# A four-layer graph network: the queries of layers 2 and 3 made with the keys and values, kept in DRAM, and loaded already replicated

## The chip, the core and the metric

The kernel runs on one core of a Trainium2 chip. The metric is the device time of one execution in microseconds; three runs of the kernel before took 2970.14 to 2981.36 us, with a median of 2976.62. The engines are called PE (TensorE, matmuls; PEld are its weight loads), DVE (VectorE), ACT (ScalarE), POOL (GpSimd) and SP (SyncE, which here only issues DMAs).

## What is computed

16 graphs share one adjacency matrix of 1024 nodes with about 8 neighbours each. Every node has 128 features in each graph, in float32. Four layers follow each other: attention (8 heads of 16) with a feed-forward part, a graph attention layer, and two more attention layers like the first.

```python
# attention layer (L0, L2, L3), for each of the 16 graphs
Q, K, V = h @ Wq, h @ Wk, h @ Wv                  # 8 heads of 16
scores = Q . K / sqrt(16), over neighbours only
attn_out = softmax(scores) @ V
x = layer_norm(h + attn_out @ Wo + bo) * ln1_g + ln1_b
y = relu(x @ W1 + b1) @ W2 + b2                   # 128 -> 256 -> 128
x = layer_norm(x + y) * ln2_g + ln2_b

# graph attention layer (L1)
h = x @ W;  e = leaky_relu(h @ a_src + (h @ a_dst)^T), over neighbours only
x = layer_norm(softmax(e) @ h + x) * ln_gamma + ln_beta
```

## The kernel before

**Units.** The nodes are sorted by degree and cut into T = 8 tiles of 128. The 16 graphs form two groups (g) of 8, and each group two halves (h) of GH = 4. A unit is one layer, group and tile; 64 units run one after another, layer by layer, group by group.

**Parts.** The work of a unit is gathering. For each tile there is a list of chunks; a chunk is 128 neighbour slots, 4 slots of 32 destination nodes each, and the 8 tiles have 17, 12, 12, 11, 8, 8, 8 and 6 chunks. In an attention layer a part is two chunks, in the graph layer four. For a part, GpSimd gathers rows of keys and values (8 graphs x 128 features x 2) from a table in DRAM with indirect DMAs (`gathered`, L746), three parts ahead, into four buffers. VectorE multiplies keys by queries (`products`, L757), adds up each head (`exponentials`, L773), ScalarE takes the exponential (L777), and VectorE multiplies the values by it (`weighted`, L798). TensorE adds the slots of a node together with 0/1 matrices (`summed`, L825).

**Queries.** Partition p of a chunk belongs to destination node p mod 32 of a block j of 32. The queries must therefore stand in SBUF four times over, `qr[32*s + n, j, :]`, for s = 0 to 3. `queries(u + 1)` does that while unit u runs. For each half: four matmuls with Wq (L718), a ScalarE copy to the tile `q` (L722), four matmuls with a 0/1 matrix that repeats 32 rows four times (L727), and four ScalarE copies of 128x512 from PSUM to `qr` (L730). The tile `q` comes from a pool with one buffer, `qr` from one with two.

**Tails.** When all parts of a unit are summed, `divided` makes the quotients, and two tails (one for each half) carry them on while the next unit's parts run: output projection, norm, feed-forward part, norm, and, in `finish`, the transposed result and `project` of the next layer. `project` stores the transposed state in DRAM (`kept`, L456; loaded again by `loaded` two units ahead), multiplies it by Wk and Wv (L464), copies the result to `kv` (L468), and stores that in the next layer's table (L473). The second half runs one step behind the first.

**Order.** Everything is emitted in an order written out by hand, with Python generators; each `yield` is one step. Each engine works through its own instructions in that order. `others()` is called three or four times for a part: it advances both tails by a step at a pace of STEPS (GRAPH_STEPS in layer 1) steps per unit, and one generator of `fronts` (queries and loads of the next units) or, if there is none, of `slow`. What is left of the tails at the end of the next unit is emitted at once (`while tails`), and so are the `fronts` at the end of each unit.

**The slow path.** While group 0 of layer 0 runs, `at_leisure(1)` makes the keys and values of group 1: for each of 16 half tiles it loads `xg` (one buffer, L620), transposes it (L522), runs `project` for layer 0 and stores the table. Before the first gather of group 1 what remains of it is emitted at once.

All DMAs from SP (loads of x, xg and weights, stores of kept and tables) are issued in one queue; the gathers are issued by GpSimd.

Of the kernel before, what the change touches and what calls it, by code (L numbers as in the profile page):

```python
# [12 lines left out]
F32 = mybir.dt.float32  # L13
# [7 lines left out]
P = 128  # L21
D = 128
# [18 lines left out]
N = 1024  # L41
T = N // P
GR = 2
G = B // GR
HF = 2
GH = G // HF
ROW = G * D
# [13 lines left out]
            CHUNK[_t, _r, _j] = len(CHUNK)  # L61
NC = len(CHUNK)

STEPS = 16
GRAPH_STEPS = 9
AHEAD = 3

# [9 lines left out]
def sparse_path(ctx: ExitStack, tc: tile.TileContext, a: dict, out: bass.AP, flag):  # L77
# [9 lines left out]
    def bank(shape):  # L87
        return banks.tile(shape, F32, tag="ps", name="ps")
# [351 lines left out]
    for l, (_, names) in enumerate(LAYERS):  # L440
# [5 lines left out]
        (l, g): dram.tile([T, P, HF, GH * P], F32, name=f"kept{l}{g}")  # L446
        for l in range(1, len(LAYERS)) for g in range(GR)
    }
    xs = {}
    srcs = {}  # L450


    def project(l, g, t, h, x, kv=None):

        if l:
            nc.sync.dma_start(kept[l, g][t, :, h, :], x.rearrange("p g n -> p (g n)"))  # L456
        table = tables[l, g][t * P : (t + 1) * P, :]
        if LAYERS[l][1] is ATTN:
            if kv is None:
                kv = twos.tile([P, 2, GH, D], F32, tag="kv", name="kv")  # L460
            for i in range(0, GH, 2):
                ps = bank([P, 2, 2 * D])
                for k in range(2):
                    nc.tensor.matmul(  # L464
                        ps[:, k, :], x[:, i + k, :], w[LAYERS[l][0], "Wkv"],
                        start=True, stop=True,
                    )
                nc.scalar.copy(  # L468
                    kv[:, :, i : i + 2, :].rearrange("p c g d -> p g c d"),
                    ps.rearrange("p g (c d) -> p g c d", d=D),  # L470
                )
                yield
            nc.sync.dma_start(  # L473
                table.rearrange("p (c x) -> p c x", c=2)[:, :, h * GH * D : (h + 1) * GH * D],
                kv.rearrange("p c g d -> p c (g d)"),
            )
            return
        kv = twos.tile([P, GH * D + GH], F32, tag="kv", name="kv")
        if h == 0:
            srcs[g, t] = const.tile([P, G], F32, name=f"src{g}{t}")  # L480
        for i in range(0, GH, 2):
            ps = bank([P, 2, D + 2])
            for k in range(2):
                nc.tensor.matmul(ps[:, k, :], x[:, i + k, :], wg, start=True, stop=True)
            nc.scalar.copy(
                kv[:, i * D : (i + 2) * D].rearrange("p (g d) -> p g d", d=D), ps[:, :, :D]
            )
            to = GH * D + i
            nc.scalar.copy(
                kv[:, to : to + 2].rearrange("p (g o) -> p g o", o=1), ps[:, :, D : D + 1]  # L490
            )
            at = h * GH + i
            nc.scalar.copy(
                srcs[g, t][:, at : at + 2].rearrange("p (g o) -> p g o", o=1), ps[:, :, D + 1 :]
            )
            yield

        nc.sync.dma_start(table[:, h * GH * D : (h + 1) * GH * D], kv[:, : GH * D])
        nc.sync.dma_start(table[:, ROW + h * GH : ROW + (h + 1) * GH], kv[:, GH * D :])
# [30 lines left out]

    def finish(l, g, t, h, z, gain, shift):
        if l + 1 < len(LAYERS):
            xn = states.tile([P, GH, P], F32, tag="xT", name="xT")
            turned(z, xn, gain, shift)
            yield
            yield from project(l + 1, g, t, h, xn)
            return
        o = twos.tile([P, GH, D], F32, tag="kv", name="outs")
        nc.gpsimd.tensor_tensor(o, z, over_graphs(gain), ALU.mult)
        nc.gpsimd.tensor_tensor(o, o, over_graphs(shift), ALU.add)  # L540
        nc.gpsimd.indirect_dma_start(
            out=out.rearrange("n (k c) -> (n k) c", k=GR * HF),
            out_offset=bass.IndirectOffsetOnAxis(ap=places[:, g, h, t : t + 1], axis=0),
            in_=o.rearrange("p g d -> p (g d)"), in_offset=None,
        )
# [59 lines left out]
    def natural(g, t, h, rows, kv=None):  # L605

        xn = states.tile([P, GH, P], F32, tag="xT", name="xT")
        turned(rows, xn)
        yield
        yield from project(0, g, t, h, xn, kv)  # L610

    def columns(g, h, n=1):
        at = (g * HF + h) * GH * D
        return slice(at, at + n * GH * D)

    def at_leisure(g):
        def fetch(k):
            rows = ones_.tile([P, GH, D], F32, tag="xg", name="xg")
            if k < T * HF:
                nc.sync.dma_start(  # L620
                    rows.rearrange("p g d -> p (g d)"),
                    a["x"][k // HF * P : (k // HF + 1) * P, columns(g, k % HF)],
                )
            return rows

        rows = fetch(0)
        yield
        for k in range(T * HF):
            steps = natural(g, k // HF, k % HF, rows)
            next(steps)  # L630
            rows = fetch(k + 1)
            yield
            yield from steps

    def at_once(g):

# [66 lines left out]
    def queries(u):  # L703

        l, g, t = units[u]
        if not is_attention(u):
            ps = bank([P, J, G])
            for j in range(J):
                nc.tensor.matmul(ps[:, j, :], rep_of(j, True), srcs[g, t], start=True, stop=True)
            ofs[u] = smalls.tile([P, J, G], F32, tag="of", name="of")  # L710
            nc.scalar.copy(ofs[u], ps)
            return
        qs[u] = reps.tile([P, J, ROW], F32, tag="qr", name="qr")
        for h in range(HF):
            q = ones_.tile([P, GH * D], F32, tag="q", name="q")
            ps = bank([P, GH, D])
            for i in range(GH):
                nc.tensor.matmul(  # L718
                    ps[:, i, :], xs[l, g, t][:, h, i, :], w[LAYERS[l][0], "Wq"],
                    start=True, stop=True,  # L720
                )
            nc.scalar.copy(q, ps.rearrange("p g d -> p (g d)"))  # L722
            yield
            pss = []
            for j in range(J):
                ps = bank([P, GH * D])
                nc.tensor.matmul(ps, rep_of(j), q[32 * j : 32 * j + 32], start=True, stop=True)  # L727
                pss.append(ps)
            for j in range(J):
                nc.scalar.copy(qs[u][:, j, h * GH * D : (h + 1) * GH * D], pss[j])  # L730
            yield
# [133 lines left out]
    def advance(gens):  # L865
        for gen in list(gens):
            if next(gen, "end") == "end":
                gens.remove(gen)

    pace = [0.0, 0.0]  # L870

    def others():
        pace[0] += pace[1]
        while pace[0] >= 1.0:
            advance(tails)
            pace[0] -= 1.0
        for gens in (fronts or slow,):
            if gens and next(gens[0], "end") == "end":
                gens.pop(0)

# [528 lines left out]
```

## Time and profile before

| | |
|---|---|
| runs of the kernel before, median (range) | 2976.62 us (2970.14 to 2981.36) |
| the profiled execution, its own time | 2966.73 us |
| span of that execution | 2965.0 us, mean granted clock 0.832 |
| busy, share of the span | PE 71%, PEld 44%, DVE 72%, ACT 48%, POOL 51% |
| chain of waits that ended last, by engine | PE 30%, ACT 11%, DVE 11%, POOL 9%, issue 7%, DMA 4% |
| DMA | 611.19 MB, mean 206 GB/s; gathers 45.1% of 16 engines, SP's transfers 11.5% |
| copies qr<-ps, L730 (all three attention layers) | 384, busy 197.5 us, mean 596 ns |
| matmuls ps<-q,rep, L727 | 768 records, busy 168.9 us |
| matmuls ps<-Wq,x, L718 | 768 records, busy 116.0 us |

In the tables of groups, a row is one line, engine and operation: the tiles, the count, busy time and mean, then the idle time of the engine just ahead of it and what ended that. A float32 matmul leaves two records. In rows of waits the three numbers are the total in us, how often, and the longest. In a timeline the first number is the start in us from the start of the span, the second how long it took, and brackets hold the idle time before it. Rows of DMA issues give the count, the size and the median time from issue to landing.

### The profile page before, as it was taken

Reading aid. Unit: us, or ns where it says so; the run is one execution under the profiler, and the core shown is the slowest. Engines: PE = TensorE matmul, PEld = TensorE weight load, DVE = VectorE, ACT = ScalarE, POOL = GpSimd, SP = SyncE. Lnnn points to the kernel's source line nnn. Section 1 sums busy time; section 2 is a strip of 40 time slices with the busy share of each in tenths; the row PEclk is TensorE's granted clock in tenths of the full one; section 3 lists DMA queues with packets and bytes.
Section 4 is the critical chain, followed back from the end, with each engine's and each line's share of the span. In section 5 each row is a group of like instructions: output and inputs, shape, how many; then the busy total and the mean of one; then the engine's idle time right before and its main releaser. Section 6 shows DMA issues by size and latency. Waiting matters only on the chain.

```text
span 2965.0 us, 35574 instructions
## 1 busy us (share of the span) xinstructions
PE 2097.9 (71%) x12692; PEld 1316.6 (44%) x12692; DVE 2141.1 (72%) x1521; ACT 1427.9 (48%) x4482; POOL 1517.5 (51%) x1096
## 2 busy tenths in 40 slices
PE   6466677767687867766587886778777676666766
PEld 5334445434454534333255553455534344334444
DVE  7876656478766566667788768886688876788772
ACT  3134455544556545345255653555644455334454
POOL 3334443354555587784254433444435566466673
PEclk8677788887788988978789988889987888777887
DMA  7655555366464577787566555565565454365540
GB/s 244 247 191 188 198 204 179 118 218 244 157 242 143 190 269 263 282 280 290 186 240 253 195 200 229 224 248 206 185 238 210 181 204 181 119 238 206 189 146 23
DMA packets 168842, 611.19 MB, mean 206 GB/s; under 512 B 44216, under 2 KB 47672, under 8 KB 120158
## 3 DMA queue, kind: packets, MB, share of 16 engines
q0 software_dynamic: 100736, 485.12, 45.1%
q1 hardware_dynamic: 67920, 123.71, 11.5%
q8 instruction: 102, 1.67, 0.2%
q14 instruction: 84, 0.69, 0.1%
HBM read 654.87 MB, written 92.34 MB: 252 GB/s over the span
## 4 chain that ended last, share of the span: by engine, by line
PE 30%; ACT 11%; DVE 11%; POOL 9%; issue 7%; DMA 4%; POOLq 0%; DVEq 0%; SPq 0%; ACTq 0%
PE ps L572 6%; ACT z L506 4%; PE yps L581 4%; PE acc L825 4%; PE ps L522 4%; POOL e L746 4%; DVE pr L798 3%; DVE sc L773 3%; POOL rstd L512 3%; DMA e<-table,idx 3%; DVE pr L757 3%; PE ps L464 2%; ACT qr L730 2%; PE yps L585 2%; PE yps L558 2%
## 5 line engine op out<-in xcount | busy, mean ns | idle before, releaser
L746 POOL DMA_INDIRECT e<-table,idx x656 | 894.3, 1363 | 456.1 <-DVE pr L798 257.8
L798 DVE TENSOR_TENSOR pr<-e,ex 128x2048 f32<-128x2048 f32 (+1 forms) x344 | 760.0, 2216 | 414.8 <-ACT ex L777 409.3
L512 POOL TENSOR_TENSOR rstd<-total,power 128x4 f32<-128x4 f32 x224 | 371.1, 1658 | 688.0 <-ACT z L506 645.8
L757 DVE TENSOR_TENSOR pr<-e,qr 128x2048 f32<-128x2048 f32 (+1 forms) x258 | 565.6, 2192 | 101.2 <-DMA e<-table,idx 62.9
L825 PE MATMUL acc<-pr,marks 128*32 128x512 f32 x2624 | 467.1, 692 | 154.3 <-DVE pr L798 143.8
L773 DVE TENSOR_REDUCE sc<-pr 128x128 f32<-128x2048 f32 (+1 forms) x258 | 561.7, 2177 | 0.0
L522 PE MATMUL ps<-ident,z 128*128 128x128 f32 x768 | 196.1, 366 | 215.2 <-ACT z L515 215.2
L522 PEld LDWEIGHTS ps<-ident,z 128*128 128x128 f32 x768 | 126.8, 172 | 360.6 <-ACT z L515 291.6
L825 PEld LDWEIGHTS acc<-pr,marks 128*32 128x32 f32 x2624 | 89.6, 119 | 408.4 <-issue 212.8
L464 PE MATMUL ps<-Wkv,xT 128*128 128x256 f32 x768 | 227.3, 440 | 57.9 <-ACT xT L524 39.5
L572 PE MATMUL ps<-x,W 128*128 128x512 f32 x384 | 240.0, 758 | 38.3 <-ACT x L526 38.3
L581 PE MATMUL yps<-W,f 128*128 128x128 f32 x1536 | 257.3, 285 | 12.8 <-ACT f L576 10.6
L581 PEld LDWEIGHTS yps<-W,f 128*128 128x128 f32 x1536 | 210.8, 195 | 69.9 <-ACT f L576 43.6
L576 ACT ACTIVATE f<-ps,b 128x512 f32<-128x512 f32 x192 | 131.4, 687 | 228.3 <-PE ps L572 227.6
L730 ACT COPY qr<-ps 128x512 f32<-128x512 f32 x384 | 197.5, 596 | 76.8 <-PE ps L727 76.6
L506 ACT ACTIVATE z<-y,root 128x128 f32<-128x128 f32 x512 | 198.5, 396 | 48.3 <-DVE y L599 37.2
L777 ACT ACTIVATE ex<-sc 128x128 f32<-128x128 f32 (+1 forms) x258 | 81.2, 315 | 287.3 <-DVE sc L773 287.1
L727 PE MATMUL ps<-q,rep 32*128 32x512 f32 x768 | 168.9, 679 | 63.8 <-ACT oT L524 39.1
L464 PEld LDWEIGHTS ps<-Wkv,xT 128*128 128x128 f32 x768 | 157.0, 218 | 99.0 <-ACT xT L524 43.0
L558 PE MATMUL yps<-Wo,oT 128*128 128x128 f32 x768 | 179.9, 321 | 8.7 <-ACT oT L524 8.7
L515 ACT ACTIVATE z<-y,rstd 128x128 f32<-128x128 f32 x512 | 162.6, 391 | 24.7 <-POOL rstd L512 24.7
L559 PE MATMUL yps<-centre,x 128*128 128x128 f32 x768 | 170.4, 309 | 0.0
(148 smaller groups left out, 2922.4 us busy)
## 6 DMA issues: line engine op xcount, KB each, us to landing
table<-kv SPq DMA_DIRECT2D x88, 512.0 KB, 9.1
kept<-xT SPq DMA_DIRECT2D x96, 256.0 KB, 5.3
x<-kept SPq DMA_DIRECT2D x48, 512.0 KB, 9.8
e<-table,idx POOLq DMA_INDIRECT x656, 7.5
table<-kv SPq DMA_DIRECT2D x32, 256.0 KB, 6.4
edges<-in_adj SPq DMA_DIRECT2D x8, 512.0 KB, 6.0
spare<-in_x SPq DMA_DIRECT2D x8, 512.0 KB, 7.7
table<-ex SPq DMA_DIRECT2D x8, 512.0 KB, 7.8
```

Of the source, the lines that this page charges most:

```text
L464: nc.tensor.matmul(ps[:, k, :], x[:, i + k, :], w[LAYERS[l][0], "Wkv"], start=True, stop=True,)
L506: nc.scalar.activation(z[:, i, :], y[:, i, :], AF.Square, scale=D**-0.5, bias=root, accum_out=total[:, i : i + 1],)
L512: nc.gpsimd.tensor_tensor(rstd, total, power, ALU.pow)
L522: nc.tensor.transpose(ps[:, i, :], z[:, i, :], ident)
L572: nc.tensor.matmul(ps, p["W1"][:, f * P : (f + 1) * P], x1.rearrange("p g n -> p (g n)"), start=True, stop=True,)
L581: nc.tensor.matmul(ps[:, i, :], f1[:, f, i * P : (i + 1) * P], p["W2"][:, f, :], start=(f == 0), stop=False,)
L730: nc.scalar.copy(qs[u][:, j, h * GH * D : (h + 1) * GH * D], pss[j])
L746: nc.gpsimd.indirect_dma_start(out=es[i][:, k, :], out_offset=None, in_=tables[l, g][:, :], in_offset=bass.IndirectOffsetOnAxis(ap=idx[:, ...
L757: nc.vector.tensor_tensor(prs[i][0][:, :n, :], es[i][:, :n, :ROW], qs[u][:, j : j + n, :], ALU.mult)
L773: nc.vector.tensor_reduce(sc[:, :n, :], prs[i][0][:, :n, :].rearrange("p k (a d) -> p k a d", d=HD), mybir.AxisListType.X, ALU.add,)
L798: nc.vector.tensor_tensor(prs[i][k0 // 2][:, :m, :].rearrange("p k (a d) -> p k a d", d=d), es[i][:, k0 : k0 + m, base : base + ROW].rearr ...
L825: nc.tensor.matmul(accums[u][32 * j : 32 * j + 32, h, :], marks[:, CHUNK[t, r, j], :], tiles[j // 2][:, j % 2, h * GH * D : (h + 1) * GH * D],
```

## The change

In layers 2 and 3 the queries are no longer made just ahead of their unit. `project`, in the tail of the layer before, multiplies its state by Wq as well, copies the result to `q` and stores it in a table `qtab` in DRAM. `queries` then fills `qr` by 16 loads of 32 rows of 4 KB, four copies of each block, issued by SP. Layer 0 makes its queries as before. STEPS goes from 16 to 17, since `project` has one more step; GRAPH_STEPS stays. Two flags are added around the slow path: `held` is set while `at_leisure` is inside a half tile, and `busy` counts the tails that are inside `finish`. `finish` first advances the slow path while `held` is set, and `others` takes the slow path only if it is inside a half tile or no tail is in `finish`.

```diff
-STEPS = 16
+STEPS = 17
...
+    qtabs = {
+        (l, g): dram.tile([N, ROW], F32, name=f"qtab{l}{g}")
+        for l, (_, names) in enumerate(LAYERS) if l and names is ATTN for g in range(GR)
+    }
...
@@ project
+            if l:
+                q = ones_.tile([P, GH * D], F32, tag="q", name="q")
+                ps = bank([P, GH, D])
+                for i in range(GH):
+                    nc.tensor.matmul(
+                        ps[:, i, :], x[:, i, :], w[LAYERS[l][0], "Wq"], start=True, stop=True
+                    )
+                nc.scalar.copy(q, ps.rearrange("p g d -> p (g d)"))
+                yield
+                nc.sync.dma_start(
+                    qtabs[l, g][t * P : (t + 1) * P, h * GH * D : (h + 1) * GH * D], q
+                )
             return
...
@@ finish
         if l + 1 < len(LAYERS):
+
+            while held[0]:
+                advance(slow)
+            busy[0] += 1
             xn = states.tile([P, GH, P], F32, tag="xT", name="xT")
             turned(z, xn, gain, shift)
             yield
             yield from project(l + 1, g, t, h, xn)
+            busy[0] -= 1
             return
...
+    busy, held = [0], [False]
+
@@ at_leisure
         for k in range(T * HF):
             steps = natural(g, k // HF, k % HF, rows)
+            held[0] = True
             next(steps)
             rows = fetch(k + 1)
             yield
             yield from steps
+            held[0] = False
...
@@ queries
         qs[u] = reps.tile([P, J, ROW], F32, tag="qr", name="qr")
+        if l:
+            for j in range(J):
+                at = t * P + 32 * j
+                rows = qtabs[l, g][at : at + 32, :]
+                for s in range(S):
+                    nc.sync.dma_start(qs[u][32 * s : 32 * s + 32, j, :], rows)
+            return
...
+    def idle():
+        return slow if held[0] or not busy[0] else []
+
     def others():
...
-        for gens in (fronts or slow,):
+        for gens in (fronts or idle(),):
             if gens and next(gens[0], "end") == "end":
                 gens.pop(0)
```

## The prediction

> **What bounds the kernel now.** I read the granted clock and span first (one core, 2965.0 us, clock 0.832), then busy time by stage. The starts of VectorE's RECIPROCAL, one per unit, give the layers: layer 0 runs to about 975 us, layer 1 to 1370, layer 2 to 2150, layer 3 to 2935. Busy time of each engine in these four stretches (PE, PEld, DVE, ACT, POOL, then the clock, the DMA share and GB/s):
>
> ```profile
> 110.00:975.00 865.00, 595.61 (x3595) 385.76 (x3595) 592.63 (x404) 412.40 (x1319) 390.57 (x266) 0.81 0.53 190
> 975.00:1370.00 395.00, 287.61 (x1948) 163.84 (x1948) 250.37 (x271) 184.77 (x636) 285.46 (x214) 0.87 0.75 262
> 1370.00:2150.00 780.00, 588.84 (x3516) 364.87 (x3516) 612.44 (x359) 421.01 (x1258) 334.39 (x249) 0.86 0.59 218
> 2150.00:2935.00 785.00, 542.07 (x3181) 333.80 (x3181) 600.86 (x340) 362.69 (x1174) 461.49 (x327) 0.82 0.49 182
> ```
>
> No engine is full. In layers 2 and 3 VectorE leads with 77 to 79%, in layer 1 the DMA engines with 75%. Next, who VectorE and ScalarE wait for; first layer 0, then layer 3:
>
> ```profile
> DVE pr L798 <- ACT ex L777: 227.0, 52, 13.7
> ACT kv L485 <- DMA table<-kv: 45.5, 5, 14.5
> ...
> DVE pr L798 <- ACT ex L777: 76.8, 32, 5.6
> DVE pr L757 <- DMA e<-table,idx: 45.8, 19, 5.5
> ```
>
> VectorE's largest wait is for the exponentials, a 0.3 us activation. It is late because ScalarE works through one queue, and copies and norms of the tail stand ahead of it. The second line is a warning for this change: a ScalarE copy stood up to 14.5 us, with all behind it, until a store had read the buffer it was to fill.
>
> One part (two chunks) costs VectorE three instructions of 2.2 us, 6.6 us. A unit of tiles 1 to 3 has 6 parts and so 39.6 + 3.2 us (reciprocal, two quotients, two sums) = 42.8 us; a unit of tiles 4 to 6 has 4 parts, 29.6 us; the measured units are 47.7 and 40 to 42 us in layer 2, 50 to 52 and 41 to 42 in layer 3. So large units hang on VectorE with 5 to 8 us of stalls, and small ones on the tail: a chain of TensorE, ScalarE and GpSimd steps spread over the unit. How the queries stand in that chain, in the timeline of a small unit of layer 3:
>
> ```profile
> 2462.45 2.05 ACT L730 COPY qr<-ps 128x512 f32<-128x512 f32 x4 [0.47 <-PE ps L727]
> ...
> 2468.16 2.02 ACT L730 COPY qr<-ps 128x512 f32<-128x512 f32 x4
> ...
> 2470.05 0.34 ACT L777 ACTIVATE ex<-sc 128x128 f32<-128x128 f32 x1
> ...
> 2479.18 0.69 ACT L576 ACTIVATE f<-ps,b 128x512 f32<-128x512 f32 x1 [3.00 <-PE ps L572]
> ...
> 2482.35 2.29 DVE L798 TENSOR_TENSOR pr<-e,ex 128x2048 f32<-128x2048 f32 x1 [3.55 <-ACT ex L777]
> ```
>
> The second group of four copies holds up the tail's next norm step by 2 us; 12 us later the tail is late, ScalarE waits 3.00 us for TensorE in it, and VectorE loses 3.55 us behind that.
>
> The boundary of two units in layer 2, where the change puts its new copies:
>
> ```profile
> 1644.54 0.21 ACT L844 COPY both<-ps 128x64 f32<-128x64 f32 x1 [2.55 <-PE ps L839]
> ...
> 1648.00 0.59 ACT L524 COPY oT<-ps 128x512 f32<-128x512 f32 x1
> ...
> 1649.33 0.31 ACT L777 ACTIVATE ex<-sc 128x128 f32<-128x128 f32 x1
> ```
>
> And what a store takes to land in layer 2 (last number, median us), and the slow path's loads in layer 0:
>
> ```profile
> table<-kv SPq DMA_DIRECT2D x32, 512.0 KB, 12.6
> kept<-xT SPq DMA_DIRECT2D x33, 256.0 KB, 5.4
> ...
> xg<-in_x SPq DMA_DIRECT2D x12, 256.0 KB, 4.1
> ```
>
> [...]
>
> **The change part by part.**
>
> *Removed in layers 2 and 3* (32 units): the repeating matmuls (16 records a unit; by stretch 53.5 us in layer 2 and 58.3 in layer 3, 3.5 us a unit) and the copies to qr (8 a unit, 66.9 and 62.0 us, 4.0 a unit). *Moved one layer up*: the Wq matmuls (16 records, 2.3 us a unit) and the copy q (two of 0.585 us) go into the tail of layers 1 and 2. Net: layer 3 loses 5.8 us of TensorE and 5.2 of ScalarE a unit, layer 2 loses the repeating part, layer 1 gains 2.3 and 1.2 us.
>
> *Layer 3.* In the unit shown, the tail reaches the scaled z of its first half earlier by 0.8 (Wq ahead of Wo on TensorE) + 0.7 (first copies ahead of the squares) + 0.6 (copy q) + 2.1 (second copies) = about 4 us. In small units I give VectorE that and half a microsecond of late sums, 4.5 us: 8 x 4.5 = 36. In tiles 1 to 3 only the one stall of about 2.7 us per unit on ex goes, the others are GpSimd's outs and gathers: 6 x 2.5 = 15. In the two large units 4 each, 8. Sum -59. Against it the loads: 16 transfers of 128 KB a unit, 2 MB. They may start when VectorE is done with the products of the unit before last, a whole unit ahead, when GpSimd is busy with outs and gathers are few. By the layer's rate when busy (182 GB/s at a share of 0.49, 371 GB/s) 2 MB are 5.7 us of all DMA engines. A landing gather may be that much later, once a unit; three parts of prefetch hide most. I take 0.7 us a unit, 11 us; bounds 0 and 5 us a unit (80). Layer 3: -48.
>
> *The new wait.* The tile q has one buffer. Both halves of a tail come one step apart, so in ScalarE's queue the second half's copy q stands one kv copy after the first half's, and must wait until the first half's q store has landed. Behind it stand the next unit's oT (the start of its tail), of, and ex; VectorE waits for these. Landing: 2.0 us at least, 5.4 as for kept[...]. I take 8 us in layer 2, 5.5 in layer 1 (there kept lands in 3.7 and the 512 KB store in 7.8).
>
> *Layer 2.* From "both" at 0: first q ready at 1.9, store issued 2.2, landed 10.2, second q 10.8, oT 11.4, ex 11.8. VectorE can use ex from 6.8 (reciprocal, quotients, reduction, products), so it loses 5 us, and the tail starts 8 us later than at 1648.00. Minus the 4 us that the queries' leaving saves in the tail: +4 in small units (8 x 4 = 32); +3.5 in tiles 1 to 3, where 1.5 is saved (6 x 3.5 = 21); +3 twice in the large ones (6). The three waits of VectorE for qr copies in this layer, 22.0 us, go but for 4: -18. Layer 2: +41; with the bounds on the landing -25 to +90.
>
> *Layer 1.* Small units (15 to 22 us) are led by the tail, whose step count GRAPH_STEPS stays at 9 although it has one yield more, so the end is flushed at the unit's border. There q waits about 5 us ahead of "of", on which VectorE's next scores depend: 8 x 5 = 40. In the other eight units VectorE waits for gathers anyway (56.5 us in the layer), and I take 1 us for q and 1 for the 0.5 MB more stored per unit: 16, less 1 hidden. Layer 1: +55; bounds +15 and +100.
>
> *Layer 0.* The flag held is set at each tile's start and cleared only when the generator is resumed, which at once sets it again for the next tile; no yield lies between. So the loop in finish does not end one tile, it drains the slow path to its end. In the changed instruction order 13 transposes of xg stand in one block on TensorE in unit 1, ahead of the first kept store. One tile's period there: transposes 1.1, issue 0.5, landing of the next xg 4.1 plus what the 512 KB store beside it takes, 6.5 us in all (5.3 with the shortest landing of 3.6, 10 with the longest, 9.1). 12 x 6.5 + 5 for the last tile - 6 that VectorE still has queued = 77 us stall. In return the other units lose this work: tiles 1 to 7 take 605.78 - 198.27 = 407.5 us in group 0 and 1003.72 - 672.43 = 331.3 in group 1, which has none: -76. Layer 0: +1; bounds -15 and +45.
>
> Sum: +1 + 55 + 41 - 48 = +49 us on the profiled execution (2966.73 us, span 2965.0), 3016. The runs' median, 2976.62, stands 10 us above that: 3026.
>
> **The rivals.** What this measurement can tell from no change is about 0.5%, 15 us.
> 1. *Relief wins* (ends faster). The q store lands in 3 to 4 us[...]; layer 1 costs 25, layer 2 gains 10, layer 3 gains 65, layer 0 gains 5: -55, 2922. It decides from a landing under 4.5 us on. For it: kept lands in 3.7 in layer 1, 2.0 at best. Against: the 512 KB store just ahead.
> 2. *The pieces cancel.* Landing about 6 us and layer 1's waits mostly behind gathers: within 15 us, 2977.
> 3. *Transfers collide with gathers.* The 2 MB a unit delay gathers by 2 us or more each unit: +64 on the forecast, 3090. For it: the DMA wait of 45.8 us in layer 3 is already there. Against: layer 1 runs at 262 GB/s with only 56.5.
> 4. *A long drain.* At 10 us a tile the block is 119 us: +42, 3068.
>
> **How the numbers follow.** Forecast (3000 to 3055) 0.37, relief 0.20, cancel 0.13, collision 0.17, long drain 0.13. Faster 0.20, same 0.13, slower 0.67. Range 2932 to 3092.
>
> **What would show it.** A stretch of 65 to 100 us in unit 1 of layer 0 with VectorE idle for ex, then units of 55 and 44 us; a wait of ScalarE's q for the qtab DMA, 32 times, 3 to 8 us; layer 1 longer by 15 to 100 us; small units of layer 3 near 37 us. I am wrong if that wait is under 3 us, if unit 1 shows no block, or if layer 3 does not shorten.

## The result, and the profile after

| | runs | median us (range) | ratio to before (95% interval) |
|---|---|---|---|
| before | 4 | 2973.80 (2970.14 to 2981.36) | |
| after | 4 | 3142.78 (3138.92 to 3157.20) | 1.0574 (1.0533 to 1.0615) |

The changed kernel is slower by 169 us. The forecast was 3026 us in a range of 2932 to 3092: the direction is right, the size is not. The profiled execution of the changed kernel took 3140.48 us, its span is 3138.7 us and the mean granted clock 0.804 (before: 0.832).

First the stages. The starts of VectorE's RECIPROCAL, one a unit, cut both traces into layers. This table gives the length of each layer in us, and the mean unit of tiles 1 to 3 and of tiles 4 to 7:

| | layer 0 | layer 1 | layer 2 | layer 3 | units of layer 2 | units of layer 3 |
|---|---|---|---|---|---|---|
| before | 1003.7 | 379.5 | 763.8 | 775.6 | 48.1 / 41.0 | 51.1 / 40.6 |
| after | 1028.7 | 435.7 | 841.6 | 789.1 | 51.5 / 46.9 | 54.3 / 39.4 |
| difference | +25.0 | +56.2 | +77.8 | +13.5 | | |
| forecast | +1 | +55 | +41 | -48 | | |

Busy time of each engine in the four layers of the kernel after (the forecast's table of the kernel before is cut at 975 and 1370 us, ahead of the borders at 1003.7 and 1383.2, so only its lines for layers 2 and 3 can be laid beside these; PE, PEld, DVE, ACT, POOL, each with its count, then granted clock, DMA share, GB/s):

```profile
110.00:1028.70 918.70, 620.25 (x3710) 403.07 (x3711) 604.06 (x412) 432.00 (x1372) 398.77 (x276) 0.82 0.51 183
1028.70:1464.40 435.70, 298.68 (x2054) 179.03 (x2054) 247.50 (x267) 185.45 (x629) 278.04 (x207) 0.83 0.73 251
1464.40:2306.00 841.60, 569.46 (x3215) 373.80 (x3214) 597.48 (x350) 345.80 (x1096) 307.67 (x243) 0.81 0.76 250
2306.00:3095.00 789.00, 484.86 (x2714) 296.32 (x2712) 600.28 (x335) 286.88 (x1010) 454.47 (x321) 0.77 0.68 222
```

In layer 3 ScalarE is busy for 76 us less than before and TensorE for 57 us less, VectorE is as busy as it was (600.28 against 600.86), and the layer is longer. So the relief reached the engines that it was meant for, and does not show in the time. The clock of layer 3 fell from 0.82 to 0.77, and the DMA share rose from 0.49 to 0.68.

Now who waits. Waits in the whole run of the kernel after, one line of ScalarE, one of VectorE, one of SP (us in total, how often, the longest):

```profile
ACT q L489 <- DMA qtab<-q: 227.7, 31, 11.6
...
DVE pr L831 <- ACT ex L810: 431.3, 107, 64.2
...
SPq L491 <- ACT q L489: 218.5, 48, 13.7
```

VectorE's waits in the same kernel, in layer 2 alone:

```profile
DVE pr L831 <- ACT ex L810: 113.7, 35, 10.2
DVE y L584 <- PE yps L581: 103.6, 22, 12.8
```

and in layer 3 alone:

```profile
DVE pr L831 <- ACT ex L810: 70.5, 24, 10.2
DVE pr L790 <- DMA e<-table,idx: 39.7, 11, 7.1
...
DVE pr L790 <- DMA qr<-qtab: 11.8, 5, 4.7
```

The forecast wait is there: ScalarE's copy to q stood for a store to land 31 times, 7.3 us in the mean (227.7 / 31). In layer 3, which has that copy in its first unit alone (two waits, 17.6 us), VectorE's wait for the exponentials is 70.5 us. Between the borders of the layer it was 84.2 before (76.8 in the forecast's window): it fell by 14 us, although ScalarE has 76 us less to do there. The longest wait for an exponential, 64.2 us, is the block in unit 1 of layer 0.

What the copy holds up, at a border of two units in layer 2. ScalarE first (start, duration, and in brackets the idle time ahead of it and its releaser), then VectorE at the same time, then SP:

```profile
1701.20 0.59 ACT L489 COPY q<-ps 128x512 f32<-128x512 f32 x1 [0.30 <-PE ps L486]
...
1714.75 0.59 ACT L489 COPY q<-ps 128x512 f32<-128x512 f32 x1 [10.26 <-DMA qtab<-q]
1715.23 0.59 ACT L541 COPY oT<-ps 128x512 f32<-128x512 f32 x1
1715.71 0.32 ACT L810 ACTIVATE ex<-sc 128x128 f32<-128x128 f32 x1
...
1708.10 2.27 DVE L806 TENSOR_REDUCE sc<-pr 128x128 f32<-128x2048 f32 x1
1719.69 0.69 DVE L584 TENSOR_TENSOR y<-yps,bo 128x512 f32<-128x512 f32 x1 [9.32 <-PE yps L581]
...
1701.81 0.33 SPq L491 DMA_DIRECT2D qtab<-q  x1
1702.68 0.52 SPq L478 DMA_DIRECT2D table<-kv  x1
1715.36 0.33 SPq L491 DMA_DIRECT2D qtab<-q  x1
1715.79 0.69 SPq L724 DMA_DIRECT2D x<-kept  x1
```

The store of the first half's q is issued at 1701.81, and the second half's copy starts 12.9 us later. ScalarE took up nothing else in its 10.26 us of idle time: the exponential came behind q and oT at 1715.71, though VectorE's sum sc, from which it is made, had ended at 1710.37 (1708.10 + 2.27). oT, the start of the next tail, stands right behind q, at 1715.23, and VectorE's sum y needs what TensorE makes of oT: VectorE stands for 9.32 us. The wait thus shows up under the name of TensorE (103.6 us of VectorE in layer 2; before, such waits were 22.9 us there), and only ScalarE's row tells its cause. SP issued the load of the next x only behind the second store, at 1715.79 after 1715.36.

### The profile page after: what moved, and what is told of

The parts are those of the page before. It is cut to its first block, busy times and chain, and to the rows that moved or that the text cites. A ratio compares the mean times of both kernels' runs of the same rounds, so it can differ in the third digit from the quotient of the medians.

```text
span 3138.7 us, 35259 instructions
## 1 busy us (share of the span) xinstructions
PE 2064.2 (66%) x12180; PEld 1327.0 (42%) x12180; DVE 2140.0 (68%) x1521; ACT 1302.3 (41%) x4226; POOL 1493.6 (48%) x1096
## 3 DMA queue, kind: packets, MB, share of 16 engines
q0 software_dynamic: 100736, 485.12, 43.9%
q1 hardware_dynamic: 101712, 207.63, 21.2%
## 4 chain that ended last, share of the span: by engine, by line
PE 26%; DMA 14%; ACT 8%; POOL 8%; issue 7%; DVE 7%; POOLq 0%; SPq 0%; DVEq 0%; ACTq 0%
DMA qtab<-q 7%; PE ps L594 5%; DMA e<-table,idx 4%; PE yps L603 4%; POOL e L779 4%; PE ps L539 4%; PE acc L858 3%; ACT z L523 3%; PE ps L469 2%; PE yps L580 2%; DVE pr L831 2%; PE yps L607 2%; POOL rstd L529 2%; DVE sc L806 2%; DVE pr L790 2%
## 5 line engine op out<-in xcount | busy, mean ns | idle before, releaser
L529 POOL TENSOR_TENSOR rstd<-total,power 128x4 f32<-128x4 f32 x224 | 339.8, 1518 | 854.2 <-ACT z L523 838.0
L858 PE MATMUL acc<-pr,marks 128*32 128x512 f32 x2624 | 489.2, 702 | 188.7 <-DVE pr L831 180.7
L580 PE MATMUL yps<-Wo,oT 128*128 128x128 f32 x768 | 202.8, 356 | 150.3 <-ACT oT L541 150.3
L603 PE MATMUL yps<-W,f 128*128 128x128 f32 x1536 | 263.3, 288 | 27.7 <-ACT f L598 25.1
L580 PEld LDWEIGHTS yps<-Wo,oT 128*128 128x128 f32 x768 | 157.9, 255 | 179.9 <-ACT oT L541 172.0
L581 PE MATMUL yps<-centre,x 128*128 128x128 f32 x768 | 190.5, 340 | 0.0
L539 PE MATMUL ps<-ident,o 128*128 128x128 f32 x384 | 76.6, 335 | 166.3 <-DVE o L882 166.3
```

The costliest lines, as they stand in the source:

```text
L529: nc.gpsimd.tensor_tensor(rstd, total, power, ALU.pow)
L539: nc.tensor.transpose(ps[:, i, :], z[:, i, :], ident)
L580: nc.tensor.matmul(ps[:, i, :], oT[:, i, :], p["Wo"], start=True, stop=False)
L603: nc.tensor.matmul(ps[:, i, :], f1[:, f, i * P : (i + 1) * P], p["W2"][:, f, :], start=(f == 0), stop=False,)
L858: nc.tensor.matmul(accums[u][32 * j : 32 * j + 32, h, :], marks[:, CHUNK[t, r, j], :], tiles[j // 2][:, j % 2, h * GH * D : (h + 1) * GH * D],
```

## The experiments

Every kernel was timed beside the kernel before on the same chip, so ratios are compared, and differences in microseconds are such a ratio applied to 2974. The first theory was that the single buffer of q makes most of the loss. Its rival was that the 2 MB of loads for each unit, or the drain of the slow path, make it.

**A second buffer for q.** The second half's q takes the buffer of xg, which lies idle after layer 0.

```diff
-                q = ones_.tile([P, GH * D], F32, tag="q", name="q")
+                q = ones_.tile([P, GH * D], F32, tag="xg" if h else "q", name="q")
```

> The changed kernel with a second buffer for q: the second half's copy takes the tile xg, which lies unused after layer 0. Theory (the wait of ScalarE's copy q for the store of the first half, 227.7 us in 31 waits of the changed kernel, is what lengthens layers 1 and 2): the wait goes, layer 1 loses 40 to 55 us and layer 2 50 to 80, in all about 3020 us. Rival (layers 1 and 2 are longer by the Wq work in the tail and by the transfers, and ScalarE had time to wait): 3115 us or more, with the wait gone and other waits of the same sum in its place.

Measured: 3016.21 us, 1.0158 (1.0140 to 1.0176). The wait for the store is gone, and 0.0416 of the ratio, 124 us, with it. Layer 2 falls from 841.6 to 757.6 us; layer 1 falls by 28.5, from 435.7 to 407.2, less than was expected. Layer 3 stays (792.6): its loss has another cause. These lengths are of the one profiled execution, which took 3036.34 us; the other four took 3014.86 to 3016.78, so they are some 20 us too long together. In return VectorE now waits for the loads. Its waits from layer 1 on, with two buffers:

```profile
DVE pr L790 <- DMA qr<-qtab: 91.8, 11, 16.7
DVE pr L831 <- ACT ex L810: 82.6, 32, 6.9
DVE pr L790 <- DMA e<-table,idx: 60.0, 18, 6.7
```

**No drain.** The kernel after without the two flags; the slow path is taken as before.

```diff
-            while held[0]:
-                advance(slow)
-            busy[0] += 1
...
-            busy[0] -= 1
...
-        for gens in (fronts or idle(),):
+        for gens in (fronts or slow,):
```

> The changed kernel with the slow path emitted as before: no flags held and busy in finish and others. Theory (the block of 13 half tiles in unit 1 of layer 0 costs 25 us net): unit 1 goes back from 120 to about 71 us, units 2 to 7 get 1 to 11 us longer each, 3118 us. Rival (layer 0 is longer for another reason, STEPS of 17 or a clock that differs): 3143 us, unit boundaries of group 0 all shifted alike.

Measured: 3146.37 us, 1.0586 (1.0555 to 1.0617), the same as with the drain. Unit 1 of layer 0 is 68.0 us long instead of 120.3 (before: 70.8), but the units after it are longer, and group 0 ends the same: 619.1 us against 621.4. The drain costs nothing here, and yet layer 0 is about 25 us longer than before in both (1028.7 and 1030.0 us). Another edit does that.

**The loads alone.** The kernel before, with no query work in layers 2 and 3; qr is filled by the same 16 loads, from rows of the keys. The queries of these layers are thus left out, and no q is made or stored.

```diff
+        if l:
+            for j in range(J):
+                at = t * P + 32 * j
+                rows = tables[l, g][at : at + 32, :ROW]
+                for s in range(S):
+                    nc.sync.dma_start(qs[u][32 * s : 32 * s + 32, j, :], rows)
+            return
```

> The kernel before, with the 16 loads a unit in layers 2 and 3 alone: the queries of these layers are left out altogether (no Wq, no repeating matmuls, no copies, no store of q), and qr is filled with 32-row pieces of the keys' table, as many bytes and transfers as in the changed kernel. It shows what the relief is worth with the loads beside it. Theory A of the prediction (relief wins over the transfers): layers 2 and 3 lose about 50 us each, 2870 us. Theory B (the 2 MB a unit delay the gathers, as the DMA waits in layer 3 of the changed kernel suggest, and eat the relief): 2940 to 2990 us, layer 3 within 20 us of before, landing of a gather near 9 us in place of 7.5.

Measured: 2977.24 us, 1.0015 (0.9994 to 1.0036). With all query work gone from TensorE and ScalarE in two layers, and nothing but loads in its place, there is no gain. Either the relief is small or the loads eat it; two later kernels tell.

**The store alone, twice without success.** Two q buffers, no drain, the store of q as in the change, and the queries made as before as well. First the tails' q shared its buffers with the queries' q. Beside the edits of the two kernels above (second buffer, no drain):

```diff
-        if l:
-            for j in range(J):
-                at = t * P + 32 * j
-                rows = qtabs[l, g][at : at + 32, :]
-                for s in range(S):
-                    nc.sync.dma_start(qs[u][32 * s : 32 * s + 32, j, :], rows)
-            return
```

> The changed kernel with two buffers for q and the old slow path, but queries made as before from x (so the product with Wq is made twice in layers 2 and 3, once for the table that nobody loads). It shows the price of making and storing q in the tail without any loads. Theory (only the one buffer is dear): layer 1 plus 20 us, layer 2 plus 20 us, layer 3 as before, 3015 us. Rival (the work in the tail itself is dear): layer 1 plus 45 or more, layer 2 plus 50 or more, 3070 us.

Measured: 3138.81 us, 1.0563 (1.0538 to 1.0587). But ScalarE's copy for the queries now waited for the tails' stores (the row is of ScalarE's waits):

```profile
ACT q L743 <- DMA qtab<-q: 106.1, 18, 9.3
```

So q was moved to a pool of two buffers that the tails' y uses, with the loads left out in the same way and the drain kept:

```diff
-                q = ones_.tile([P, GH * D], F32, tag="q", name="q")
+                q = twos.tile([P, GH * D], F32, tag="y", name="q")
```

> Queries made as before in layers 2 and 3, beside a q made in the tail of the layer before and stored in a table that nobody loads; this q takes the two buffers of y, so that it meets neither the queries' q nor its own other half. The price of making and storing q alone (the Wq product is made twice in layers 2 and 3). Theory: layer 1 plus 25 us (as with two buffers: 407 against 380), layer 2 plus 25, layer 3 as before, 3030 us with the slower layer 0. Rival (the 863 us of layer 2 in the run with a shared q were the tail's own work): 3100 or more.

Measured: 3114.63 us, 1.0483 (1.0455 to 1.0512), and now VectorE's sums y wait for the stores:

```profile
DVE y L621 <- DMA qtab<-q: 117.5, 19, 13.9
...
DVE y L584 <- DMA qtab<-q: 68.9, 19, 9.4
```

Neither isolates the cost of a store. In both, the tile that shared its buffer with one that a store reads took over the wait, on the engine that wrote it next: ScalarE in the first (106.1 us in 18 waits), VectorE in the second (186.4 us in 38, the two rows together).

**Fewer, larger loads.** Two q buffers, and 4 loads of 512 KB for a unit instead of 16 of 128 KB.

```diff
-            for j in range(J):
-                at = t * P + 32 * j
-                rows = qtabs[l, g][at : at + 32, :]
-                for s in range(S):
-                    nc.sync.dma_start(qs[u][32 * s : 32 * s + 32, j, :], rows)
+            rows = qtabs[l, g][t * P : (t + 1) * P, :].rearrange("(j n) c -> n j c", n=32)
+            for s in range(S):
+                nc.sync.dma_start(qs[u][32 * s : 32 * s + 32, :, :], rows)
```

> Two buffers for q, as in the run that gave 3016 us, and qr filled by 4 loads of 512 KB a unit in place of 16 of 128 KB, the same bytes. Theory (number of transfers: SP waits for the landing of earlier loads 135 times, 120.2 us, so that the 16 come in two waves and late; VectorE waits 91.8 us for qr in that run): the qr wait falls below 30 us and the time to about 2970. Rival (bytes: the DMA engines' share is 0.88 in layer 2 and 0.71 in layer 3): within 15 us of 3016, gathers no earlier.

Measured: 3090.83 us, 1.0395 (1.0358 to 1.0433), 70 us worse than with 16 loads (1.0395 - 1.0158). That is neither the 2970 us of the theory nor the 3016 of the rival. The DMA issues of this kernel (count, size, median us to landing), and then VectorE's waits in it:

```profile
qr<-qtab SPq DMA_DIRECT2D x128, 512.0 KB, 23.0
...
DVE pr L788 <- DMA e<-table,idx: 132.0, 37, 9.7
DVE pr L788 <- DMA qr<-qtab: 107.8, 10, 21.7
```

VectorE waits 107.8 us for the loads (91.8 with 16 of them) and 132.0 for gathers (73.4 with 16). The 23.0 us can't be laid beside the 9.3 of the small loads: one is the landing of a quarter of the unit's queries, the other of a sixteenth. How SP issues them for the same unit of layer 2 (start, duration), first with 16 loads, then with 4:

```profile
1664.28 26.14 SPq L745 DMA_DIRECT2D qr<-qtab  x16
```

```profile
1672.08 4.36 SPq L743 DMA_DIRECT2D qr<-qtab  x4
```

With 16 loads SP waits again and again for earlier ones to land (182.7 us in 166 waits), so that the loads are spread out; with 4 all 2 MB are under way almost at once. Counted by the bytes that SP's queue had moved, all of a unit's queries had landed 22.4 us after the first issue with 16 loads and 24.5 us after it with 4 (estimates from the two traces, medians of 32 units). So the queries come hardly later; the wait that grew most is that for gathers. That the bunched loads hold the gathers up fits this, but was not tested. Fewer issues were no help.

**The old pace.** Two q buffers and STEPS = 16.

```diff
-STEPS = 17
+STEPS = 16
```

> Two buffers for q and STEPS back at 16. Theory (the faster pace of the tails is what lengthens layer 0 by 25 us, since its tails have no step more): layer 0 back to about 1005 us, in all 2990. Rival (pace doesn't matter): layer 0 near 1030, in all 3016.

Measured: 2997.26 us, 1.0092 (1.0060 to 1.0124). The pace alone is worth 0.0066, 20 us, between the theory and the rival; the intervals of 16 and 17 do not overlap, though barely. By layer (two buffers, STEPS 17 and then 16): layer 0 1034.4 and 1017.3, layer 1 407.2 and 397.5, layer 2 757.6 and 768.7, layer 3 792.6 and 771.5 (the first of each pair from the long execution named above). STEPS is raised for the extra step in `project`, but the tails of layers 0 and 3 do not have that step: they only run faster, and those are the layers that lose. Why a tail that ends sooner makes a unit longer was not taken further.

**The repeating matmuls put back, unread.** Two q buffers, and in layers 2 and 3 the 16 repeating matmul records a unit run again on x; nobody reads their result. It asks whether the lower clock, not the work, eats the relief.

```diff
+            for h in range(HF):
+                yield
+                for j in range(J):
+                    ps = bank([P, GH * D])
+                    nc.tensor.matmul(
+                        ps, rep_of(j),
+                        xs[l, g, t][32 * j : 32 * j + 32, h].rearrange("p g n -> p (g n)"),
+                        start=True, stop=True,
+                    )
+                yield
```

> Two buffers for q, loads as in the changed kernel, and the repeating matmuls kept in layers 2 and 3 with another operand (x in place of q), their results read by nobody: 512 matmul records more than in the run that gave 3016 us, no copies. Theory (TensorE's freed time is given back by a lower granted clock: matmul busy fell by 34 us where 512 records of 218 ns, 112 us, left): busy rises by under 60 us, granted clock back toward 0.83, time within 15 us of 3016 or below. Rival (TensorE's work was on the path): 3050 or more.

Measured: 3029.34 us, 1.0224 (1.0181 to 1.0266), 20 us more than without them: neither within the 15 us of the theory nor as much as the rival's 3050. TensorE's busy time in the page of two buffers, and then in the page with the matmuls back:

```profile
PE 2058.8 (68%) x12180; PEld 1307.3 (43%) x12180; DVE 2142.4 (71%) x1521; ACT 1309.1 (43%) x4226; POOL 1520.9 (50%) x1096
```

```profile
PE 2109.3 (70%) x12692; PEld 1330.6 (44%) x12692; DVE 2139.8 (71%) x1521; ACT 1308.8 (43%) x4226; POOL 1494.5 (50%) x1096
```

512 more records make TensorE busy for 50.5 us more; in the kernel before, the 512 records of these layers took 114.1 (2.3 + 53.5 + 58.3, the first in the forecast's stretch of layer 1). The profiled clocks are 0.814 and 0.830, but other executions of the kernel with two buffers had 0.820 to 0.825, so part of this is scatter. Putting the work back bought no time.

**The relief alone.** The kernel before with no query work in layers 2 and 3 and no loads: the two qr tiles of layer 0 are used again. The queries of these layers are left out.

```diff
+        if l:
+            qs[u] = qs[2 * T - 1 - u % 2]
+            return
```

> The kernel before without any work for the queries of layers 2 and 3: no Wq, no repeating matmuls, no copies, and no loads; the units take the two qr tiles that layer 0 filled last. It shows the whole relief. Prediction's terms: layer 3 minus 59 us, layer 2 about minus 55 with the qr waits, 2855 us. Rival (the relief was never there: TensorE's lower granted clock and other waits take it): 2940 us or more. Beside the run with the loads alone (2977 us) the difference is the price of 64 MB of loads in place.

Measured: 2942.19 us, 0.9887 (0.9856 to 0.9918). All that the change could take from layers 2 and 3, in this order of instructions, is worth 34 us, 17 in each. VectorE's waits in layer 3 of this kernel:

```profile
DVE pr L801 <- ACT ex L780: 70.5, 27, 7.1
DVE pr L760 <- DMA e<-table,idx: 42.3, 18, 5.1
```

In the kernel before, between the borders of the same layer:

```profile
DVE pr L798 <- ACT ex L777: 84.2, 33, 7.3
DVE pr L757 <- DMA e<-table,idx: 45.8, 19, 5.5
```

The wait for exponentials gives back 13.7 us of the 59 that were forecast for this layer; in layer 2 it gives back nothing (103.0 us before, 105.5 here), and what goes there are the waits for qr and some of those for TensorE. A small unit of layer 3 without any query work shows what else an exponential is late for:

```profile
2424.80 3.05 POOL L512 TENSOR_TENSOR rstd<-total,power 128x4 f32<-128x4 f32 x1
...
2427.89 1.14 ACT L515 ACTIVATE z<-yps,rstd 128x128 f32<-128x128 f32 x4 [3.90 <-POOL rstd L512]
2428.90 0.33 ACT L780 ACTIVATE ex<-sc 128x128 f32<-128x128 f32 x1
...
2429.26 3.32 DVE L801 TENSOR_TENSOR pr<-e,ex 128x2048 f32<-128x2048 f32 x1 [2.31 <-ACT ex L780]
...
2433.92 1.12 PE L522 MATMUL ps<-ident,o 128*128 128x128 f32 x4 [9.18 <-DVE o L852]
...
2436.30 0.63 PE L559 MATMUL yps<-centre,x 128*128 128x128 f32 x2
...
2441.17 0.39 PE L559 MATMUL yps<-centre,x 128*128 128x128 f32 x2
```

The exponential stands behind a norm step (z, L515) that waits 3.90 us for GpSimd's rstd, here a 3.05 us instruction; the copies for queries are gone, and VectorE loses 2.31 us all the same. The last lines show a second thing: after 9.18 us with nothing to do, TensorE takes 0.63 us for a pair of matmuls that takes 0.39 us five microseconds later. The granted clock was 0.50 and 0.52 in the two stretches from 2434 to 2440 us, and 1.00 from 2440 to 2444. The tail that starts there starts slowly.

**Half of the loads.** As the relief alone, plus 8 of the 16 loads (64 partitions of qr are filled from rows of the keys, the others are left as they are).

```diff
+            qs[u] = qs[2 * T - 1 - u % 2]
...
+                for s in range(2):
+                    nc.sync.dma_start(qs[u][32 * s : 32 * s + 32, j, :], rows)
```

> As the run without query work, with 8 of the 16 loads a unit (two of the four copies), 32 MB in place of 64; the other two copies keep what layer 0 left. If the price of the loads goes with the bytes: midway between the run without loads and 2977 us. If it comes from the second wave of eight (SP waiting for landings) or from VectorE waiting for the last of qr: close to the run without loads, within a quarter of the way.

Measured: 2964.01 us, 0.9958 (0.9942 to 0.9974). With 0, 8 and 16 loads a unit, so 0, 32 and 64 MB in all, the ratio is 0.9887, 0.9958 and 1.0015: 21 us for the first half, 17 for the second (the last of the three kernels ran on another chip than the other two). The price is not in the second wave of eight; it grows about evenly with what is loaded. Bytes and transfers were halved together here, so this does not tell one from the other.

**Making and storing q, without loads.** Two q buffers, STEPS = 16, drain and stores as in the change; `queries` uses the two qr tiles of layer 0 again, so the stored queries are not used.

```diff
-            for j in range(J):
-                at = t * P + 32 * j
-                rows = qtabs[l, g][at : at + 32, :]
-                for s in range(S):
-                    nc.sync.dma_start(qs[u][32 * s : 32 * s + 32, j, :], rows)
+            qs[u] = qs[2 * T - 1 - u % 2]
```

> STEPS of 16 and two buffers for q, with q made in the tail and stored, but no loads: the units of layers 2 and 3 take the two qr tiles that layer 0 filled last, and the stored table is read by nobody. Beside the run without any query work the difference is the price of making and storing q with a free buffer. Theory: layer 1 plus 18 us, layer 2 plus 10 to 20, layer 3 the same: 30 to 40 us above that run. Rival (the store's landing still blocks something, as with the buffers of y): 80 or more above.

Measured: 2965.88 us, 0.9955 (0.9941 to 0.9968). This is the isolation that failed twice above: against the relief alone, making and storing q with free buffers costs 0.0068, 20 us, less than the 30 to 40 of the theory, most of it in layer 1 (397.0 us against 381.8) and, with the drain, in layer 0 (1011.9 against 1004.8).

**A faster pace in the graph layer.** Two q buffers, STEPS = 16, GRAPH_STEPS = 10. The forecast held that with 9 steps the end of a tail is flushed at the border of the unit and costs there.

```diff
-GRAPH_STEPS = 9
+GRAPH_STEPS = 10
```

> STEPS of 16 and two buffers for q (2997 us), with GRAPH_STEPS at 10. Theory (layer 1's tail has one step more and its end is flushed at the unit's border): layer 1 loses half of its 18 us, 2988. Rival (layer 1 is longer by the work of Wq itself): 2997 within 5 us.

Measured: 3047.43 us, 1.0238 (1.0201 to 1.0274), 43 us worse than with 9. Layer 1 goes from 397.5 to 447.9 us, its small units from 21.0 to 25.8. The faster pace costs far more than it can save at the border, and leaving GRAPH_STEPS alone was the better choice. Neither expectation came true, and why the pace costs so much stays open.

## Why the prediction failed

The kernel before and five others stand in a row, each one step on from the one ahead of it. Lengths of layers in us, and the ratio:

| | L0 | L1 | L2 | L3 | ratio | step, us |
|---|---|---|---|---|---|---|
| before | 1003.7 | 379.5 | 763.8 | 775.6 | 1 | |
| no query work in layers 2 and 3 | 1004.8 | 381.8 | 747.0 | 758.1 | 0.9887 | -34 |
| + q made and stored (two buffers), drain | 1011.9 | 397.0 | 751.2 | 759.2 | 0.9955 | +20 |
| + 16 loads a unit | 1017.3 | 397.5 | 768.7 | 771.5 | 1.0092 | +41 |
| + STEPS 17 | 1034.4 | 407.2 | 757.6 | 792.6 | 1.0158 | +20 |
| + one buffer for q (the change) | 1028.7 | 435.7 | 841.6 | 789.1 | 1.0574 | +124 |

The steps add up to the measured ratio because each row is measured against before; in another order they could have other sizes. Only the loads were measured twice: without any store they cost 38 us (1.0015 - 0.9887). The layers are coarser than the ratios. They come from one execution each, on several chips: the first fifteen units of layer 1 are the same instructions in four kernels (before, relief alone, half of the loads, loads alone), and took 351.7 to 362.9 us. So 10 us in one layer are scatter, and the row with STEPS 17 is the long execution.

- **The new wait: right.** It came 31 times (32 foretold): 6.7 us in the mean in layer 1 (87.1 / 13) and 7.7 in layer 2 (122.9 / 16), where 5.5 and 8 us were taken. In layer 2 the forecast held +100 us for it (64 + 30 + 6, before the relief is taken off), and the second buffer gave back 84. The 8 us lie between the 5.4 us in which 256 KB landed in layer 2 of the kernel before and the 12.6 us of 512 KB there; that the store of q would stand behind a 512 KB one was the author's assumption, and was not shown. With one buffer it landed in 5.7 to 9.2 us, 6.4 in the median. What the wait holds up is in the timeline above: 10.26 us of ScalarE, with oT 0.48 us and ex 0.96 us behind the copy.
- **The relief: the step that failed.** The forecast took 59 us for layer 3 and the same sum in layer 2 (32 + 9 + 18). Measured are 17 and 17. The working counted the ScalarE and TensorE time that left the tail, about 4 us, as time that VectorE gets back. But with all of it gone, VectorE's wait for exponentials fell by 13.7 us in layer 3 and not at all in layer 2, and the small units of layer 3 went from 40.6 to 39.4 us, and not to near 37. The one unit shown has an exponential late behind GpSimd's rstd; that this holds for most units was not shown, though ScalarE's wait for rstd in this layer did not fall either (32.3 us before, 39.1 with the relief alone). TensorE's matmuls are a second candidate: those with Wo took 337 ns in the mean with the relief alone and 321 before (last section). How much each takes stays open. That layer 3 does not shorten was named beforehand as a sign of being wrong: it is 13.5 us longer.
- **The loads: under-priced.** They were to cost 11 us, in layer 3 alone, with three parts of prefetch as the cover; for layer 2 they had no term of their own. They cost 38 to 41 us: 17.5 in layer 2 and 12.3 in layer 3 by the table, 19.0 and 22.6 in the kernels without a store. One place was overlooked, the last unit of layer 1, during which the first queries of layer 2 are loaded. It took 20.4 us without loads and 37.1 with them (in the table the other units of that layer, shorter by as much on another chip, hide it), and in the loads-only kernel VectorE stands there for one load:

```profile
DVE pr L764 <- DMA qr<-table: 17.7, 1, 17.7
```

  The forecast's rate, 5.7 us of all DMA engines for 2 MB, makes 182 us in 32 units, of which a fifth came through. Rival 3 had them at 75 (11 + 64), so the truth lay midway. Layer 1 with its 262 GB/s was no proof of cover for the landing of the queries themselves: with two buffers VectorE waited 91.8 us for them.
- **STEPS: not priced at all.** The change's text names the pace, and the forecast gave it no term. It cost 20 us by the ratio; in the profiled executions layer 0 is 17 us longer with it and layer 3 is 21, and layer 2 is 11 shorter. It is what made layer 0 25 us longer: with STEPS 17 and no drain layer 0 took 1030.0 us, with STEPS 16 and no drain 1003.7.
- **Layer 1: right by luck.** Forecast +55, measured +56. In it the single buffer is 28.5 us and not 48, and making and storing q about 15. The rest was not in the forecast: the pace of STEPS makes the first unit, with tails of layer 0, 7 us longer (40.1 before, 47.1 after), and the last one waits for the first loads (27.7 us before, 38.4 after). The reason given with the number, a flush at the border, found no support with GRAPH_STEPS = 10.
- **The drain: seen, and nearly neutral.** The block stands in unit 1 (64.2 us of waiting for one exponential, 120.3 us against 68.0 without it), and the later units give it back. In layer 0, with STEPS 16, the kernels with the drain took 1011.9 to 1017.3 us and those without 1000.9 to 1007.7; with STEPS 17 it made no difference. So the net of +1 was nearly right with both its terms too large: the block is 52 us and not 77, and 36 to 54 come back, not 76.

The sum of it: relief 118 foretold and 34 measured, +84; loads 11 and 41, +30; STEPS +20; against that wait, store and drain 156 foretold (100 + 55 + 1) and 144 measured (124 + 20), -12. The forecast of +49 becomes +171, which is 0.0574 of 2974.

No version met here that makes and uses the queries is faster than the kernel before; those below 1 leave them out. With a second buffer, the old pace and all else as in the change, the time is 1.0092 of before, since 34 us of relief stand against 61 for the store and the loads.

## What to carry to other kernels

Before a tile becomes the source of a store, count its buffers against the writes that come within one landing time (6.4 us here in the median), and read what stands behind the next write in that engine's queue (oT and ex here, after 10.26 us of idle time); the second buffer alone was worth 124 us. Busy time taken off an engine need not come back as time: layer 3 has 76 us less of ScalarE and 57 us less of TensorE than before, and the whole relief was 34 us where 118 were foretold. So measure the whole relief first, by leaving the work out, before building what is to replace it. Replication by transfer moves the bytes to the DMA engines, and the gathers use the same 16: in the kernel after, gathers took 43.9% of the time of these engines and SP's transfers 21.2% (before: 45.1% and 11.5%). The price grew with what was loaded (21 us for the first 32 MB, 17 for the next), and the same bytes in a quarter of the transfers cost 70 us more, not less.

## What the runs showed of the hardware

- **The granted clock was lower where TensorE had less work.** With all query work of layers 2 and 3 gone, the granted clock was 0.804 to 0.808 in four executions, against 0.825 to 0.835 in the 37 of the kernel before beside them. In the two kernels that store q and make the queries as before too it was 0.826 to 0.829. The amount of work is not all: with the same matmuls and two buffers it was 0.814 to 0.825 with STEPS 17 and 0.805 to 0.816 with 16, on two chips. The removed matmuls had taken 190 us by their rows (114.1 for the repeating ones, 76.4 for those with Wq), and TensorE's busy time fell by 111 (2097.9 to 1986.6). The same matmuls with Wo show the rest; the rows are from the page before, the page of the relief alone, and the page after (busy us, mean ns):

```profile
L558 PE MATMUL yps<-Wo,oT 128*128 128x128 f32 x768 | 179.9, 321 | 8.7 <-ACT oT L524 8.7
```

```profile
L558 PE MATMUL yps<-Wo,oT 128*128 128x128 f32 x768 | 190.6, 337 | 86.1 <-ACT oT L524 82.6
```

```profile
L580 PE MATMUL yps<-Wo,oT 128*128 128x128 f32 x768 | 202.8, 356 | 150.3 <-ACT oT L541 150.3
```

  Between the transposes and these matmuls the query work had stood. The idle time ahead of them grew from 8.7 to 86.1 and 150.3 us, and with it the mean of the same instruction, from 321 to 337 and 356 ns. In the unit of the relief alone shown above, the granted clock was 0.50 and 0.52 in the stretches from 2434 to 2440 us, behind 9.18 us of idle time, and 1.00 from 2440 to 2444, and the pair of matmuls took 0.63 us in the first and 0.39 in the second. Why the clock is granted so was not shown. TensorE's busy time fell by 79 us less than the rows of the removed matmuls had held (190 - 111), and the row with Wo alone is 10.7 us longer (190.6 - 179.9).
- **Larger loads beside gathers did not help.** 4 loads of 512 KB for a unit, on 32 partitions each, made the kernel 70 us slower than 16 of 128 KB: the queries had landed at about the same time (24.5 and 22.4 us after the first issue, estimates from the traces), and VectorE's waits for gathers rose from 73.4 to 132.0 us.
- **A store's landing is no constant.** The 256 KB of q landed in 6.4 us (median of the nine stores that the trace tells) with one buffer and in 10.7 with two. The loads need not be the reason: in the first kernel of the store alone, which has two buffers and no loads, it was 10.6.
